# Graph sums on one Trainium2 core: the one-hot becomes the weights, and four chunks gather into one buffer

## The chip, the core and the metric

The kernel runs on one core of a Trainium2 chip. The core has five engines with their own instruction queues: TensorE for matrix products (PE; its weight loads are shown apart as PEld), VectorE (DVE), ScalarE (ACT), GpSimd (POOL) and SyncE (SP). PE reads SBUF and writes PSUM[...]. DMAs move data between HBM and SBUF. Engines wait for each other through semaphores.

The metric is the device time of one execution in microseconds (us), lower is better. Timed runs are made without the profiler; the profile is of one more execution.

## The reference

The reference is two layers of a graph network on 6250 nodes of 256 features. The edge list has 106,250 entries, sorted by destination; both directions of 50,000 random pairs and one loop for each node.

```python
xn = _layernorm(x)
x = x + _L0_gnn_ref(xn, edge_index, ...) + _L0_mix_ref(xn[None], ...)[0]   # two graph convolutions; linear attention
x = x + _L0_ffn_ref(_layernorm(x)[None], ...)[0]                           # 8 experts, the best one a node
xn = _layernorm(x)
x = x + _L1_gnn_ref(xn, ..., src, dst) + _L1_mix_ref(xn[None], ...)[0]      # mean of neighbours; attention and MLP
x = x + _L1_ffn_ref(_layernorm(x)[None], ...)[0]                            # shared MLP, 4 experts, the best two
```

Three times (two convolutions of layer 0, one mean in layer 1) it needs, for each node, the sum of the rows of its neighbours:

```python
msg = h[src] * norm[:, None]
out = jax.ops.segment_sum(msg, dst, num_segments=num_nodes)
```

In layer 0 a node's own row is added too (a second loop on top of the one in the edge list), and the sum is multiplied by a 256 x 256 matrix.

## The kernel before

**Tiles and chunks.** Nodes are held in 49 tiles of 128 (`NT`), 256 features each. Edges are worked on in 831 chunks of 128 (`NCH`), in the order of their destinations. As these are sorted, 17 chunks (`PER`) make up about one tile of destinations, and `base_of(c)` (L79) tells where chunk c's destinations should begin.

**Three passes.** `neighbour_sums` (L530) is called three times, at L826, L1148 and L1564, with the tables t1, t2, t3 in HBM. Each table has the nodes' rows in float32 (1 KB a row); t2 and t3 have them also as three bf16 parts that add up to the float32 value (1.5 KB a row). For each chunk POOL issues an indirect DMA (L542) that gathers the 128 source rows into SBUF, into `rows` or `parts`. Which of the two is settled by `is_f32` (L58): pass one is all float32; pass two has float32 in its first 136 chunks and in each third group of four after that, 367 in all; pass three in each fourth group, 208 chunks. Each chunk has a buffer of its own. `depth` tells how many there are: 12 float32 in pass one, 12 and 8 (bf16) in pass two, 6 and 10 in pass three.

**The one-hot.** For each group of four chunks (`OG`) DVE compares a row of numbers with the chunk's destinations `lof` (L549). The result has, for each edge, a one in the column of its destination, in a window of 84 nodes (`WIN`) that begins 38 (`MARG`) below `base_of(c)`.

**The products.** At L567 the gathered rows are the weights (128 edges by 128 features, two halves), and the one-hot is streamed through with its 84 columns. So the sums come out transposed: features on partitions, nodes on columns. A float32 chunk takes 2 products, a bf16 chunk 6. They add into a PSUM bank that covers one tile and 84 nodes of the next (`REACH`). As windows overlap freely, the bank is cleared first by a product with zeros (L560). In passes one and two the node's own rows are added by two products with the identity (L574), of a tile `own` that SP loads (L556).

**After a tile's last chunk** `whole` (L581) brings the bank into SBUF: ACT copies the part that only this tile's chunks reached (L587), DVE adds to the first 84 columns what the bank before had left over (L588), ACT keeps what belongs to the next tile (L592). The result is already transposed and goes as weights into the next product (`product`, L758, or the neigh product of `feed`, L1441).

**The order.** PE, POOL and SP run in the order in which the program is written; DVE and ACT are ordered by the compiler's scheduler. A planner, `pace` (L595), mixes other work into the three passes. It keeps a clock of its own: each chunk has a slot of 1.25 us, of which the sums are charged 0.45 (float32) or 0.23 (bf16) (L579), times a factor of 1.0 to 1.2. In the rest of the slot it places parts of other jobs. A job is a generator; `yield a, b` says that the part cost a of the slot's time and that the next may come b later. What is not placed by the last chunk is placed behind it by `rest()`. The jobs are:

- pass one: `settle1` (product and activation of a finished tile, which writes t2), the attention of layer 0 (`attention`), clearing of memory;
- pass two: `settle2`, `route` (gate of the 8 experts; scatters rows into `xs` by an indirect DMA on POOL, L947), `serve` (loads 1 MB of an expert's weights per chunk of 128 nodes, `hidden` and L1058, and scatters the result into `ys` on POOL, L1070), `back` (writes t3). Pass three cannot begin before t3 is complete;
- pass three: `mixing` (attention and MLP, fc1 and fc2), `feed` (mean of neighbours, experts, output).

The scatters into `xs` and `ys` stand in POOL's queue between the gathers. The first waits for slots from DVE, the second for y from DVE.

**The general branch.** If a destination lies outside its chunk's window (`far`, L422), a slow branch computes the sums another way. It decides at run time.

Of the kernel before, what the change touches and what calls it, by code (L numbers as in the profile page):

```python
# [31 lines left out]
F32 = mybir.dt.float32  # L33
# [21 lines left out]
FORMS = (1, 3, 4)  # L55


def is_f32(form, c):  # L58
    return c // OG % FORMS[form] == 0 or (form == 1 and c < 8 * PER)


# [12 lines left out]
MARG = 38  # L74
WIN = 84
# [7 lines left out]
def window(c):  # L83
    b = base_of(c) - MARG
    return max(b, 0), min(b + WIN, NPAD)


def tile_of(c):

    return window(c)[0] // P  # L90
# [3 lines left out]
REACH = P + WIN  # L94


OWN = (3, 13)
FINAL = [max(c for c in range(NCH) if tile_of(c) == t) for t in range(NT)]
AW = 7


def abase(c):

    return (base_of(c) - MARG) // 16
# [38 lines left out]
def gps_kernel(ctx: ExitStack, tc: tile.TileContext, i: dict, out: bass.AP):  # L143
# [57 lines left out]
    nc.vector.tensor_scalar(iota_w, iota_f, float(MARG), None, op0=ALU.subtract)  # L201
    iota_wf = consts.tile([P, P], F32, name="iota_wf")
    nc.vector.tensor_scalar(iota_wf, iota_f, float(MARG), None, op0=ALU.subtract)
    zrow = consts.tile([P, 512], BF16, name="zrow")
    nc.vector.memset(zrow, 0.0)
# [120 lines left out]
    with ExitStack() as st:  # L326
# [23 lines left out]
        for j in range(PER):  # L350
            nc.gpsimd.memset(offs[:, 0, j:j + 1], float(base_of(j)))
            nc.gpsimd.memset(offs[:, 1, j:j + 1], float(abase(j)))
# [6 lines left out]
        alo = alo.rearrange("p a b -> p (a b)")  # L359
        zb = prep.tile([P, 8 * NT], BF16, name="zb")  # L360
# [38 lines left out]
        for c0 in range(0, NCH, P):  # L399
# [7 lines left out]
            for c in range(c0, c0 + n):  # L407
                a, b = max(abase(c), 0), min(abase(c) + AW, 8 * NT)
                nc.tensor.matmul(dg[:, a:b], lhsT=ob[:, c - c0, :],
                                 rhs=oa[:, c - c0, a - abase(c):b - abase(c)],  # L410
                                 start=False, stop=(c == NCH - 1), skip_group_check=True)
# [13 lines left out]
        nc.vector.tensor_scalar(far[:, :NCH - 1], lof[:, :NCH - 1], WIN / 2.0 - MARG - 0.5, None, op0=ALU.subtract)  # L425
        nc.vector.tensor_scalar(far[:last, NCH - 1:], lof[:last, NCH - 1:], WIN / 2.0 - MARG - 0.5, None,
# [9 lines left out]
        nc.vector.tensor_scalar(fall, fall, WIN * WIN / 4.0, None, op0=ALU.is_gt)  # L436
# [93 lines left out]
    def neighbour_sums(tables, form, gp, after, own, other, depth=(8, 8)):  # L530
# [7 lines left out]
        for c in range(NCH):  # L538
            f32 = is_f32(form, c)
            g = gp.tile([P, C if f32 else 3 * C], F32 if f32 else BF16, name="rows" if f32 else "parts",  # L540
                        bufs=depth[0 if f32 else 1])
            nc.gpsimd.indirect_dma_start(  # L542
                out=g, out_offset=None, in_=(table if f32 else parts)[:, :],
                in_offset=bass.IndirectOffsetOnAxis(ap=sp[:, c:c + 1], axis=0))
            if c % OG == 0:
                n = min(OG, NCH - c)
                ohs = gp.tile([P, OG, WIN], F32 if f32 else BF16, name="onehotf" if f32 else "onehot",
                              bufs=4 if f32 and form < 2 else 3)
                nc.vector.tensor_tensor(ohs[:, :n, :],  # L549
                                        (iota_wf if f32 else iota_w)[:, None, :WIN].to_broadcast([P, n, WIN]),  # L550
                                        lof[:, c:c + n, None].to_broadcast([P, n, WIN]), op=ALU.is_equal)
            oh = ohs[:, c % OG, :]
            if own and c % PER == 0 and c // PER < NT:
                T = c // PER
                owns[T] = gp.tile([P, C], F32, name="own", bufs=2)
                nc.sync.dma_start(owns[T], table[T * P:(T + 1) * P, :])  # L556
            b = tile_of(c)
            if b not in ps:
                ps[b] = banks["pool"].tile([P, 512], F32, name="sums", tag="sum", bufs=2)
                nc.tensor.matmul(ps[b][:, :2 * REACH], lhsT=zrow[:, :P], rhs=zrow[:, :2 * REACH],  # L560
# [1025 lines left out]
```

## Time and profile before

| | us |
|---|---|
| timed runs, median of 3 (4121.96 to 4128.04) | 4127.97 |
| profiled execution | 4857.88 |
| its span, first to last instruction | 4856.1 |
| first gather | 98.7 |
| pass one, first to last gather | 98.7 to 1315.4 |
| pass two | 1339.5 to 2885.4 |
| pass three | 3306.7 to 4746.5 |

The profiled execution is 730 us longer than the timed ones. The granted TensorE clock is 0.815 on average, lowest in pass one. How the page shows the stages, in 40 slices of 121 us, in tenths:

```profile
PE   3787557567576567758667678865778877878878
POOL 2666666666555565555555541104555555555550
PEclk9898676666667678878788789987888888998989
DMA  4455334333332354444444543655333333333330
```

A digit is the busy share of the slice (for PEclk the granted clock, for DMA the mean of 16 engines). The three stretches of 5 and 6 in POOL's row are the passes.

In the lists of instructions, a float32 product shows as two records, a bf16 product as one. `x5624` is the number of records; the number behind the bar is the time in which at least one was running, then the mean of one, then the idle time of the engine before them with what ended it. A wait put down to "remote" ended by a signal that the profile ties to no instruction near it.

### The profile page before, as it was taken

What the parts mean: (1) busy time and instruction counts of PE and PEld (TensorE: products, weight loads), DVE (VectorE), ACT (ScalarE), POOL (GpSimd) and SP (SyncE); (2) the same over time, 40 slices, a digit from 0 to 9 for tenths busy, and PEclk for the clock granted to TensorE, in tenths of its full rate; (3) what the DMA queues carried; (4) which work ended last, traced back from release to release, by engine and by line L of the source; (5) the groups of instructions that cost most, each with busy time, mean ns of one, the idle gap of its engine ahead of it and who ended that gap; (6) DMA issues with size and microseconds to landing.
All of it is one profiled execution on the core that took longest, in us unless ns stands there. A gap on an engine that the chain in (4) does not pass through costs nothing. (4 is left out here: it accounts for less than half of the span.)

```text
span 4856.1 us, 59500 instructions
## 1 busy us (share of the span) xinstructions
PE 3463.1 (71%) x22273; PEld 2860.7 (59%) x22273; DVE 1422.3 (29%) x5275; ACT 957.1 (20%) x2026; POOL 2532.2 (52%) x2665
## 2 busy tenths in 40 slices
PE   3787557567576567758667678865778877878878
PEld 2677446556565455646555456654666666666666
DVE  5312112122212222222122311733333333333333
ACT  3111000000001112212222133530112211211212
POOL 2666666666555565555555541104555555555550
PEclk9898676666667678878788789987888888998989
DMA  4455334333332354444444543655333333333330
GB/s 150 137 161 153 112 114 117 114 113 115 109 91 84 104 158 136 137 147 121 150 142 128 161 122 114 210 192 147 110 113 111 106 108 106 109 111 109 105 111 19
DMA packets 332191, 601.89 MB, mean 124 GB/s; under 512 B 57498, under 2 KB 230341, under 8 KB 331888
## 3 DMA queue, kind: packets, MB, share of 16 engines
q0 software_dynamic: 142672, 412.98, 29.5%
q1 hardware_dynamic: 188366, 184.56, 12.4%
q8 instruction: 176, 2.88, 0.2%
q14 instruction: 127, 1.04, 0.1%
q10 hardware_dynamic: 850, 0.43, 0.0%
HBM read 521.95 MB, written 75.80 MB: 123 GB/s over the span
## 5 line engine op out<-in xcount | busy, mean ns | idle before, releaser
L567 PE MATMUL sums<-onehotf,rows 128*128 128x84 f32 (+2 forms) x5624 | 937.8, 313 | 273.8 <-issue 92.5
L567 PEld LDWEIGHTS sums<-onehotf,rows 128*128 128x128 f32 x5624 | 909.5, 230 | 378.9 <-issue 201.3
L542 POOL DMA_INDIRECT rows<-t1f,sp x831 | 807.7, 972 | 498.7 <-issue 159.6
L542 POOL DMA_INDIRECT parts<-t3b,sp x623 | 600.0, 963 | 575.9 <-PE sums L567 325.5
L567 PEld LDWEIGHTS <-parts 128*128 128x128 bf16 x6522 | 408.3, 108 | 368.5 <-DMA parts<-t2b,sp 165.6
L567 PE MATMUL sums<-onehot,parts 128*128 128x84 bf16 x6522 | 474.4, 216 | 183.5 <-DMA parts<-t2b,sp 144.0
L542 POOL DMA_INDIRECT parts<-t2b,sp x464 | 446.6, 963 | 270.2 <-PE sums L567 98.4
L884 PE MATMUL hid<-ft,fw 128*128 128x256 f32 (+1 forms) x1824 | 522.4, 424 | 41.8 <-ACT ht L886 32.7
L549 DVE TENSOR_TENSOR onehotf<-iota_wf,lof 128x336 f32<-128x336 f32 x352 | 178.3, 508 | 1030.9 <-PE sums L567 510.5
L542 POOL DMA_INDIRECT rows<-t2f,sp x367 | 350.6, 955 | 144.8 <-issue 98.5
L884 PEld LDWEIGHTS hid<-ft,fw 128*128 128x128 f32 x1824 | 353.5, 211 | 96.6 <-ACT ht L886 39.1
L762 PE MATMUL h<-w,aggt 128*128 128x256 f32 x392 | 155.6, 535 | 238.7 <-issue 154.2
L1070 POOL DMA_INDIRECT ys<-y,to x64 | 63.9, 998 | 496.9 <-DVE y L1063 209.0
L886 ACT ACTIVATE ht<-hid,fb 128x256 f32<-128x256 f32 (+1 forms) x456 | 208.4, 471 | 458.5 <-PE hid L884 239.1
L1058 PE MATMUL exp<-wd,ht 128*128 128x256 f32 x1024 | 274.0, 408 | 5.8 <-ACT ht L886 3.6
L549 DVE TENSOR_TENSOR onehot<-iota_w,lof 128x336 bf16<-128x336 bf16 x272 | 137.1, 505 | 478.6 <-PE sums L567 225.6
L762 PEld LDWEIGHTS h<-w,aggt 128*128 128x128 f32 x392 | 92.5, 261 | 261.7 <-issue 162.3
L542 POOL DMA_INDIRECT rows<-t3f,sp x208 | 201.0, 966 | 63.2 <-issue 61.4
L1058 PEld LDWEIGHTS exp<-wd,ht 128*128 128x128 f32 x1024 | 194.3, 202 | 34.4 <-ACT ht L886 5.8
L587 ACT COPY aggt<-sums 128x88 f32<-128x88 f32 x96 | 22.3, 232 | 893.7 <-remote 422.5
L1411 PE MATMUL fc_ps<-fc,ut 128*128 128x256 f32 x588 | 166.5, 408 | 9.3 <-issue 9.1
L1399 PE MATMUL fc_ps<-ht,fc 128*128 128x256 f32 (+1 forms) x600 | 163.3, 395 | 2.0 <-issue 1.9
(356 smaller groups left out, 4540.9 us busy)
## 6 DMA issues: line engine op xcount, KB each, us to landing
wd<-in_L_ffn_Wd SPq DMA_DIRECT2D x64, 1024.0 KB
xs<-zero SPq DMA_DIRECT2D x8, 1799.0 KB
rows<-t1f,sp POOLq DMA_INDIRECT x831
parts<-t3b,sp POOLq DMA_INDIRECT x623
t2b<-t2s SPq DMA_DIRECT2D x49, 192.0 KB
t3b<-t3s SPq DMA_DIRECT2D x24, 384.0 KB
fs<-xs SPq DMA_DIRECT2D x64, 128.5 KB
bd<-in_L_ffn_bd SPq DMA_DIRECT2D x64, 128.0 KB
```

What stands on the lines that cost most here:

```text
L542: nc.gpsimd.indirect_dma_start(out=g, out_offset=None, in_=(table if f32 else parts)[:, :], in_offset=bass.IndirectOffsetOnAxis(ap=sp[:, c ...
L549: nc.vector.tensor_tensor(ohs[:, :n, :], (iota_wf if f32 else iota_w)[:, None, :WIN].to_broadcast([P, n, WIN]), lof[:, c:c + n, None].to_b ...
L567: nc.tensor.matmul(ps[b][:, h, n0 - b * P:n1 - b * P], lhsT=g[:, k * C + h * P:k * C + (h + 1) * P], rhs=oh[:, n0 - w0:n1 - w0], start=Fal ...
L587: nc.scalar.copy(dst[:, :, WIN:], sums[:, :, WIN:P])
L762: nc.tensor.matmul(h, lhsT=at[:, k, :], rhs=w[:, k, :], start=(k == 0), stop=(k == 1))
L884: nc.tensor.matmul(h_ps[:, :w], lhsT=fw1[:, k, m * P:(m + 1) * P], rhs=ft[:, k, :w], start=(k == 0), stop=(k == 1))
L886: nc.scalar.activation(ht[:, m, :w], h_ps[:, :w], AF.Gelu, bias=fb1[:, m:m + 1], scale=1.0)
L1058: nc.tensor.matmul(y_ps, lhsT=ht[:, m, q * P:(q + 1) * P], rhs=wd[:, m, :], start=(m == 0), stop=(m == 7))
L1070: nc.gpsimd.indirect_dma_start(out=ys[v][:, :], out_offset=bass.IndirectOffsetOnAxis(ap=to, axis=0), in_=y, in_offset=None)
L1399: nc.tensor.matmul(u_ps[:, :w], lhsT=fc1[:, k, m * P:(m + 1) * P], rhs=ht[:, k, :w], start=(k == 0), stop=(k == 1))
L1411: nc.tensor.matmul(h_ps, lhsT=ut[:, m, t * P:(t + 1) * P], rhs=fc2[:, m, :], start=False, stop=(m == 5))
```

## The change

The roles of rows and one-hot are exchanged, and the groups are gathered as a whole.

- A chunk's one-hot is 128 edges by 128 nodes and is the weight; the gathered rows are streamed through, 256 columns at a time. The sums come out with nodes on partitions. A float32 chunk takes one product, a bf16 chunk three (with the same weights).
- A chunk's stretch of 128 nodes begins at a multiple of 64. A PSUM bank has two halves of 256 columns: one for the tile's own stretch, one for the stretch that begins 64 nodes later. The first chunk of a stretch starts its accumulation, so that no product with zeros is needed.
- `whole` adds up the pieces with DVE and ACT, adds the own rows there (`own` is no longer a product), and `turn` transposes the tile by two PE transposes and an ACT copy before it goes on as weights. `settle1`, `settle2` and `feed` have a step for that, with 0.45 a tile in the planner's clock.
- Four chunks gather into one tile of SBUF, with four indirect DMAs issued together at the group's first chunk. `depth` counts such groups: 4 in pass one, 3 in passes two and three. The buffer comes free when the fourth chunk is done.
- Pass one is all float32, passes two and three are all bf16.
- The planner is charged 0.43 for a float32 chunk and 0.33 for a bf16 chunk.
- The offsets of the stretches need 12 more memsets on POOL before pass one; the window of the degree count is one column wider; the general branch is adapted. Pass one's buffers are in a pool of their own, which is closed after it.

```diff
-FORMS = (1, 3, 4)
 def is_f32(form, c):
-    return c // OG % FORMS[form] == 0 or (form == 1 and c < 8 * PER)
+    return form == 0
...
-MARG = 38
-WIN = 84
+HALF = P // 2
+BELOW = 60
...
 def window(c):
-    b = base_of(c) - MARG
-    return max(b, 0), min(b + WIN, NPAD)
+    return min(max((base_of(c) - BELOW + HALF // 2) // HALF * HALF, 0), (NT - 1) * P)
...
-            g = gp.tile([P, C if f32 else 3 * C], F32 if f32 else BF16, name="rows" if f32 else "parts",
-                        bufs=depth[0 if f32 else 1])
-            nc.gpsimd.indirect_dma_start(
-                out=g, out_offset=None, in_=(table if f32 else parts)[:, :],
-                in_offset=bass.IndirectOffsetOnAxis(ap=sp[:, c:c + 1], axis=0))
             if c % OG == 0:
                 n = min(OG, NCH - c)
-                ohs = gp.tile([P, OG, WIN], F32 if f32 else BF16, name="onehotf" if f32 else "onehot",
-                              bufs=4 if f32 and form < 2 else 3)
+                gs = gp.tile([P, OG, C if f32 else 3 * C], F32 if f32 else BF16, name="rows" if f32 else "parts",
+                             bufs=depth)
+                for j in range(n):
+                    nc.gpsimd.indirect_dma_start(
+                        out=gs[:, j, :], out_offset=None, in_=(table if f32 else parts)[:, :],
+                        in_offset=bass.IndirectOffsetOnAxis(ap=sp[:, c + j:c + j + 1], axis=0))
+                ohs = gp.tile([P, OG, P], F32 if f32 else BF16, name="onehotf" if f32 else "onehot", bufs=3)
...
-            for h in range(2):
-                for k in range(1 if f32 else 3):
-                    nc.tensor.matmul(ps[b][:, h, n0 - b * P:n1 - b * P],
-                                     lhsT=g[:, k * C + h * P:k * C + (h + 1) * P], rhs=oh[:, n0 - w0:n1 - w0],
-                                     start=False, stop=True, skip_group_check=True)
-            if own and c % PER == 8 and c // PER < NT:
-                T = c // PER
-                mine = owns.pop(T)
-                for h in range(2):
-                    nc.tensor.matmul(ps[T][:, h, :P], lhsT=mine[:, h * P:(h + 1) * P], rhs=ident,
-                                     start=False, stop=True, skip_group_check=True)
+            h = C * (window(c) // HALF % 2)
+            parts_n = 1 if f32 else 3
+            for k in range(parts_n):
+                nc.tensor.matmul(ps[b][:, h:h + C], lhsT=ohs[:, c % OG, :], rhs=g[:, k * C:(k + 1) * C],
+                                 start=(c in FIRST and k == 0), stop=(c in LASTS and k == parts_n - 1))
...
-            other(c, 0.45 if f32 else 0.23)
+            other(c, 0.43 if f32 else 0.33)
...
-    def whole(dst, sums, begun, last):
+    def whole(dst, sums, begun, own, last):
...
+        if own is None:
+            nc.scalar.copy(dst, sums[:, :C])
         else:
-            nc.scalar.copy(dst[:, :, WIN:], sums[:, :, WIN:P])
-            nc.vector.tensor_tensor(dst[:, :, :WIN], sums[:, :, :WIN], begun, op=ALU.add)
...
+            nc.vector.tensor_tensor(dst, own, sums[:, :C], op=ALU.add)
+        left = None
+        if not last:
+            left = gp.tile([P, C], F32, name="left", bufs=2)
+            nc.scalar.copy(left[:HALF, :], sums[HALF:, C:])
+            nc.vector.tensor_tensor(dst[HALF:, :], dst[HALF:, :], sums[:HALF, C:], op=ALU.add)
+        if begun is not None:
+            nc.vector.tensor_tensor(dst[:HALF, :], dst[:HALF, :], begun[:HALF, :], op=ALU.add)
         return left
+
+    def turn(at, agg):
+        tr = ps_tr("aggtr")
+        for k in range(2):
+            nc.tensor.transpose(tr[:, k * P:(k + 1) * P], agg[:, k * P:(k + 1) * P], ident)
+        nc.scalar.copy(at, tr[:, :C].rearrange("p (k n) -> p k n", k=2))
...
+    def settle1(T, agg):
+        yield 0.0, 2.5
         at = gp.tile([P, 2, P], F32, name="aggt", bufs=2)
+        turn(at, agg)
+        summed.pop(0)
+        yield 0.45, 1.0
...
-        neighbour_sums(t1, 0, gp, after1, True, other, depth=(12, 0))
+        neighbour_sums(t1, 0, gp, after1, True, other, depth=4)
...
-        neighbour_sums(t2, 1, gp, after2, True, other, depth=(12, 8))
+        neighbour_sums(t2, 1, gp, after2, True, other, depth=3)
...
-        at = agt[t0 // 2]
+        at = work.tile([P, 2, 2, P], F32, name="agt", bufs=2)
+        for t in range(n):
+            turn(at[:, t, :, :], agt[t0 // 2][:, t, :])
+        del agt[t0 // 2]
+        yield 0.45 * n, 1.0
...
-        neighbour_sums(t3, 2, gp, after3, False, other, depth=(6, 10))
+        neighbour_sums(t3, 2, gp, after3, False, other, depth=3)
```

## The prediction

> **What bounds the kernel now.** I read the page's busy line first, then the gathers' own line of code, then windows by stage, then the timeline inside a stage, and last the rows by shape.
>
> ```profile
> PE 3463.1 (71%) x22273; PEld 2860.7 (59%) x22273; DVE 1422.3 (29%) x5275; ACT 957.1 (20%) x2026; POOL 2532.2 (52%) x2665
> ...
> L542 POOL DMA_INDIRECT rows<-t1f,sp x831: 940/946/1390, 98.7 to 1315.4; - x167
> L542 POOL DMA_INDIRECT parts<-t3b,sp x623: 940/946/1278, 3313.0 to 4746.5; - x156
> L542 POOL DMA_INDIRECT parts<-t2b,sp x464: 940/946/1311, 1562.6 to 2881.7; - x155
> L542 POOL DMA_INDIRECT rows<-t2f,sp x367: 940/946/1270, 1339.5 to 2885.4; - x184
> L542 POOL DMA_INDIRECT rows<-t3f,sp x208: 942/946/2023, 3306.7 to 4724.9; - x104
> ```
>
> No engine is near full by busy time. But the gathers give three passes of 831: 98.7 to 1315.4 (1217 us), 1339.5 to 2885.4 (1546 us), 3306.7 to 4746.5 (1440 us). Everything else is 98.7 before, 24 and 421 between, 110 after: 654 us. The timeline tells what paces a pass:
>
> ```profile
> 691.49 0.94 POOL L542 DMA_INDIRECT rows<-t1f,sp  x1 [0.30 <-remote]
> 692.73 0.95 POOL L542 DMA_INDIRECT rows<-t1f,sp  x1 [0.30 <-issue]
> 693.98 0.95 POOL L542 DMA_INDIRECT rows<-t1f,sp  x1 [0.30 <-issue]
> ...
> 699.93 0.23 ACT L587 COPY aggt<-sums 128x88 f32<-128x88 f32 x1 [18.32 <-remote]
> ...
> 700.58 2.07 PE L762 MATMUL h<-w,aggt 128*128 128x256 f32 x4 [11.06 <-DVE aggt L588]
> ...
> 690.00:695.00 5.00, 0.00 (x0) 0.00 (x0) 0.00 (x0) 0.00 (x0) 3.78 (x4) 0.57 0.37 105
> 695.00:700.00 5.00, 0.00 (x0) 0.00 (x0) 0.51 (x1) 0.07 (x1) 2.98 (x3) 0.50 0.27 79
> ```
>
> A gather is 0.95 us and is followed by 0.30 us whatever it waits for, so POOL needs 1.25 us for each: 831 x 1.25 = 1039 us a pass, 3116 us for three. The profiled passes are 1087 us over that. The last four lines show why I don't take these 1087 us at their word: PE has run all its matmuls by 690 and idles at half clock, yet ACT and POOL are told of them one by one until 699.9. In this execution PE's signals come late. Its own time is 4857.88 us (span 4856.1 and 1.8 around it), 730 more than the median of the timed runs, 4127.97. If the 654 us outside the passes are the same without the profiler, the timed passes take 4128 - 656 = 3472 us, 356 over POOL's floor. So the timed kernel is bound by POOL's gathers in the passes and by PE and its chains in the two tails, where no gather runs:
>
> ```profile
> 2890.00:3310.00 420.00, 309.87 (x1379) 242.09 (x1378) 173.56 (x837) 166.16 (x348) 46.96 (x50) 0.90 0.51 163
> ...
> 4760.00:4856.00 96.00, 75.39 (x355) 62.53 (x353) 37.05 (x149) 29.20 (x57) 0.00 (x0) 0.91 0.03 10
> ```
>
> The sums below are made on the profiled stages; where a stage is a pass I say what of it I believe is left in timed runs, and I add the result to the median.
>
> **What the Trainium skill says.** "TensorE: Matmul & The Clock Gate", section "Back-to-back issue gap": a warm matmul of 256 columns takes 262 cycles, 109 ns. No bf16 matmul of 256 columns is in this trace; twelve float32 records of that width take 2.84 us (0.24 each, or 0.22 without the last one's drain: twice the figure, as for two passes). The same page, table at its head: PE takes weight loads ahead, GpSimd is a strict FIFO. The trace agrees: the ys scatters hold the gathers behind them. "DMA: Bandwidth & Descriptors", "Anatomy of one DMA": about 2 us fixed per DMA; here a gather issued at 2007.75 let PE go at 2015.35, beside two loads of 1 MB. "ScalarE: Activation LUTs", "What ACT_TABLE_LOAD costs": 1283 ns; the trace has 1283.
>
> **The change part by part.**
>
> ```profile
> L567 PE MATMUL sums<-onehotf,rows 128*128 128x84 f32 x5536 | 920.4, 312 | 198.9 <-issue 92.1 <-DMA rows<-t2f,sp 68.1 <-DMA rows<-t1f,sp 35.1
> L567 PE MATMUL sums<-onehot,parts 128*128 128x84 bf16 x6492 | 472.6, 216 | 183.5 <-DMA parts<-t2b,sp 144.0 <-issue 38.4
> L549 DVE TENSOR_TENSOR onehotf<-iota_wf,lof 128x336 f32<-128x336 f32 x350 | 177.4, 508 | 1018.8 <-PE sums L567 498.3 <-remote 380.5 <-issue 63.0
> ...
> L947 POOL DMA_INDIRECT xs<-f,slots x40 | 40.6, 1016 | 78.1 <-DVE slots L943 40.3 <-issue 18.5 <-DMA xs<-f,slots 10.1
> L1070 POOL DMA_INDIRECT ys<-y,to x31 | 31.2, 1008 | 192.4 <-DVE y L1063 74.8 <-DVE run L933 71.4 <-DVE pf L984 21.2
> ```
>
> (1) PE's products. Warm, a timeline row has 56 float32 records of 84 columns in 6.38 us, 0.114 each, four a chunk: 0.46 us; six bf16 ones 0.39 us with the last one's drain, I take 0.23. Before: 1406 float32 chunks x 0.46 + 1087 x 0.23 = 647 + 250 = 897, with 147 clearing products (0.18) and 392 records for own rows (0.114): 968 us. After: 831 chunks x 2 x 0.22 = 366, 1662 x 3 x 0.109 = 543, 294 transposes at 0.11 to 0.25 = 32 to 73: about 960. So 26% fewer instructions but no less array time. Both lie under POOL's 1.25 us a chunk: 0.
>
> (2) The gathers' number and pace stay: 0. They carry more: 367 + 208 = 575 chunks go from 131 to 197 KB, 38 MB in all. Below nothing is excluded. If all of it were uncovered at the 123 GB/s of the page it would be 306 us; POOL's pace covers it except where 1 MB loads run beside it. I take 10, in the second pass.
>
> (3) Four gathers stand together at the group's first chunk. In the built order a ys scatter follows its expert product by 2.4 chunks before, 3.9 after: PE's operands for it were asked for 1.5 x 1.25 = 1.9 us earlier relative to the scatter. The profiled second pass has 270 us of scatter waits (last two rows), about 30 of them long. 30 x 1.9 = 57; bounds 0 (PE late for another reason) and 95 (all 50 scatters or pairs). Fewer scatters in the pass, 28 and 38 for 31 and 40: 5 x 1.3 = 6. I take -56.
>
> (4) Buffers: 20 and 16 single ones become 12 in three groups, freed by the fourth chunk, so POOL may lead PE by 8 to 12 chunks, 10 to 15 us. PE's waits for DMA reach 9 us in the second pass. 0 to 40; I take 10. The first pass goes from 12 to 16: 0.
>
> (5) DVE and ACT. A one-hot is 512 instead of 336 elements: 508 ns becomes 0.69 to 0.77 us, 624 of them, +110 to +165 us of DVE, which is 29% busy: hidden. A tile's sums pass three more short DVE operations, two transposes and an ACT copy, some 2 us, before its product; the planner leaves 2.5 + 1.0 there. It is bare only at the end of pass one: +2. In pass three the transposes share one PSUM buffer with all others and wait for ACT's copy, about 1 us twice for 25 feeds in a pass where PE is the nearest second: 0 to 50, I take 20. Table loads rise from 226 to 268 (30 to 70 at the gelu of L1401): 42 x 1.28 = 54 us of ACT, mostly idle; I take 5. Twelve memsets of 88 ns on POOL lie in its 88.8 us wait.
>
> (6) The order. The planner charges 0.33 for a bf16 chunk where it charged 0.23 or 0.45, and 0.45 a tile for the transposes. So other work is placed later. In the built order PE has 741 matmuls between the last sum of pass two and the first of pass three before, 821 after; behind the last sum of pass three 188 before, 352 after (two more mixings and feeds). Nothing covers these: the gathers are over. First tail: 420 us for 741; 80 x 310/741 (PE busy) = 33, 80 x 420/741 = 45. I take 38. Second: 96 us for 188; 164 x 75/188 = 66, 164 x 96/188 = 84. I take 72. The passes they leave don't get shorter, since POOL paces them.
>
> Sum: 10 - 56 + 10 + 2 + 20 + 5 + 38 + 72 = +101, of which the pass terms (-9) are unsure in size and sign. 4128 + 101 = 4229; I take 4220, since the tails' extra work can overlap a little better than the work there now.
>
> **Rivals.**
> A. The passes are bound by PE's stream of instructions and its late signals in timed runs too. For it: POOL waits 567 us for sums at L542 in the profile, and a quarter of PE's instructions go. Against: the timed kernel is 730 us shorter, so little of that is left. If most of the 356 us over the floor fell (-220), with (3) and the tails: 4128 - 220 - 56 + 110 + 20 = 3982; with half of that 4090. It decides once the passes lose over 110 us, the tails' price. This is the faster side.
> B. The tails are repaid: pass three is PE's, not POOL's (it has some 930 to 940 us of PE work against 1039), so work put off shortens it. Then of the second tail only the 45 us remain by which PE's total in stage three grows: 4128 + 38 + 45 - 56 + 20 = 4175; if the first tail is repaid too, about 4137.
> C. Gathers become late: 12 buffers and 197 KB with the 1 MB loads beside them. Half of the 306 us of (2) with the 40 of (4) shows: 4229 + 140 + 30 = 4400; a quarter, 4325.
> D. The fixed stretch doesn't hold the nodes and the general branch runs. The inputs' sorted destinations lie at 0 to 117 of each stretch of 128: excluded.
>
> **Numbers.** My forecast 0.60, A 0.19 (4090 and below), B 0.09, C 0.12. What this kernel's measurement can tell from no change is about 0.2%, 8 us. Slower: forecast, C, and most of B: 0.77. Same: 0.04 from B and the edge of A. Faster: 0.19. The range drops half of A and the upper half of C: 4090 to 4325. The forecast's own is 4160 to 4280.
>
> **What would show it.** In the changed profile: gathers again every 1.25 us; PE matmul records about 16,600 with array time in the sums nearly the same; the profiled span may fall by more than the timed run, as fewer PE signals are late (so its passes must not be read alone). Step 6: time from the last gather of pass two to the first of pass three 421 + 38, from the last gather to the end 110 + 72. Step 3: ys and xs waits in pass two down from 270 towards 200. I am wrong if the tails have not grown, or if the passes lose more than 110 us in timed runs; C is seen as PE idle ended by DMA of parts in passes two and three.

## The result, and the profile after

| | us | runs |
|---|---|---|
| before, median | 4126.1 (4121.96 to 4128.04) | timed beside it |
| after, median | 4324.33 (4313.78 to 4331.61) | 4 |
| ratio | 1.048 [1.0456, 1.0504] | |

The changed kernel is 198 us slower. The forecast was 4220, which is 94 us slower.

Chips differ in this work: the kernel before takes 4113 to 4126 us on some and about 4875 us on another, so times are compared on one chip only, as ratios. The profile of before shown ahead of the prediction (4857.88 us, granted clock 0.815) looks like the slower kind: the timed runs there take 4854 to 4896 us at 0.816 to 0.822. So I took one more profile of it on a chip where it takes 4116 us. That one, not the first, stands beside the profile of after. Here are its gathers, from the view of one line's instructions (count, shortest/median/longest in ns, first and last start in us):

```profile
L542 POOL DMA_INDIRECT rows<-t1f,sp x831: 940/946/1378, 99.2 to 1164.0; - x167
L542 POOL DMA_INDIRECT parts<-t3b,sp x623: 940/946/1460, 2902.1 to 4008.3; - x156
L542 POOL DMA_INDIRECT parts<-t2b,sp x464: 942/946/1283, 1362.3 to 2467.8; - x155
L542 POOL DMA_INDIRECT rows<-t2f,sp x367: 942/946/1280, 1182.2 to 2471.5; - x184
L542 POOL DMA_INDIRECT rows<-t3f,sp x208: 942/946/2022, 2895.8 to 3993.8; - x104
```

And the same view of the changed kernel:

```profile
L542 POOL DMA_INDIRECT rows<-t1f,sp x831: 940/946/1472, 99.4 to 1181.2; - x167
L542 POOL DMA_INDIRECT parts<-t2b,sp x831: 942/946/1602, 1201.6 to 2429.4; - x167
L542 POOL DMA_INDIRECT parts<-t3b,sp x831: 942/946/1632, 2874.4 to 4139.5; - x167
```

The median gather takes the same 946 ns with 131 KB and with 197 KB. The first and last starts give the stages of both. A pass goes from its first to its last gather; the first tail is what lies between passes two and three, the second what lies behind pass three:

| stage, us | before (span 4118.0) | after (span 4312.0) | difference |
|---|---|---|---|
| ahead of the first gather | 99.2 | 99.4 | 0 |
| pass one | 1064.8 | 1081.8 | +17 |
| between | 18.2 | 20.4 | +2 |
| pass two | 1289.3 | 1227.8 | -62 |
| first tail | 424.3 | 445.0 | +21 |
| pass three | 1112.5 | 1265.1 | +153 |
| second tail | 109.6 | 172.5 | +63 |

The differences add up to the spans' 194 us. The changed kernel profiled once more, on the same chip as this profile of before, gives +22, -56, +25, +157 and +65 for the passes and tails in their order. The tails were forecast at +38 and +72. What was not forecast is pass three. The page of after shows where in it the time goes, in the last quarter of POOL's row of 40 slices (108 us each), where POOL gathers only about half as often, and PE's clock sinks with it:

```profile
POOL 1777777777767777777776411137777776544410
PEclk9999777777767798888897999979999999887789
```

POOL issues the gathers, and waits for nothing else in that stretch but the products. From the view of waits of after, 3500 to 4140 us (engine, tile and line waiting, for what; us in total, times, longest):

```profile
POOL parts L542 <- PE sums L560: 207.0, 11, 34.7
```

Nine of these eleven hold 202 us, less the 0.30 us that follows every gather anyway. They come every 55 to 76 us, once for each pair of tiles. The timeline of PE around the end of one of them, and under it POOL's:

```profile
3886.57 1.03 PE L1536 MATMUL ffn<-ew,e2t 128*128 128x256 f32 x4
3887.43 1.89 PE L1370 MATMUL att<-wf,xnt 128*128 128x256 f32 x8
3889.16 0.38 PE L587 MATMUL aggtr<-ident,agg 128*128 128x128 f32 x2
3890.01 0.44 PE L587 MATMUL aggtr<-ident,agg 128*128 128x128 f32 x2 [0.47 <-ACT agt L588]
3890.28 3.77 PE L560 MATMUL sums<-parts,onehot 128*128 128x256 bf16 x33
3894.74 0.49 PE L560 MATMUL sums<-parts,onehot 128*128 128x256 bf16 x3 [0.70 <-DMA parts<-t3b,sp]
```

```profile
3891.70 0.95 POOL L542 DMA_INDIRECT parts<-t3b,sp  x1 [30.89 <-PE sums L560]
3892.95 0.94 POOL L542 DMA_INDIRECT parts<-t3b,sp  x1 [0.30 <-issue]
```

Before 3890 PE does products of experts, mixing and feed, at full clock, and no sums: from 3860 to 3892 it is busy 30.3 of 32 us. All this while the 12 gather buffers are full, so POOL stands still for 30.89 us. Then PE takes eleven chunks in one go (33 records in 3.77 us), POOL starts again, and now PE waits for each gather. First one engine stands and then the other.

The lumps stand in the order of the program. In the trace of after nine stretches between two chunks' sums in pass three take 14 to 42 us, filled with other PE products; the longest such stretch in before takes 4.3 us. The code that makes them is unchanged: `after3` runs the planner's `step` for as long as more than two pairs of sums are waiting for `feed` (`while len(agt) > 2`). As I read it, with the new charges `feed` is always behind, so that this loop, once a pair, runs a whole lump.

### The profile page after: what moved, and what is told of

It reads as the page before. It is cut to its first block, busy times and chain, and to the rows that moved or that the text cites. A ratio compares the mean times of both kernels' runs of the same rounds, so it can differ in the third digit from the quotient of the medians.

```text
span 4312.0 us, 47268 instructions
## 1 busy us (share of the span) xinstructions
PE 3340.2 (77%) x16530; PEld 2425.5 (56%) x16530; DVE 1661.0 (39%) x5515; ACT 1064.4 (25%) x2117; POOL 2568.3 (60%) x2677
## 5 line engine op out<-in xcount | busy, mean ns | idle before, releaser
L560 PE MATMUL sums<-parts,onehot 128*128 128x256 bf16 x4986 | 891.6, 302 | 436.7 <-DMA parts<-t2b,sp 269.5
L542 POOL DMA_INDIRECT parts<-t3b,sp x831 | 807.4, 972 | 458.0 <-issue 223.0
L542 POOL DMA_INDIRECT parts<-t2b,sp x831 | 810.4, 975 | 274.8 <-issue 230.7
L560 PEld LDWEIGHTS <-onehot 128*128 128x128 bf16 x4986 | 518.4, 106 | 756.1 <-issue 556.7
L560 PE MATMUL sums<-rows,onehotf 128*128 128x256 f32 x1662 | 648.1, 503 | 283.1 <-DMA rows<-t1f,sp 225.5
L560 PEld LDWEIGHTS sums<-rows,onehotf 128*128 128x128 f32 x1662 | 337.9, 235 | 537.8 <-DMA rows<-t1f,sp 365.3
L546 DVE TENSOR_TENSOR onehot<-iota_w,lof 128x512 bf16<-128x512 bf16 x416 | 286.3, 689 | 602.9 <-PE sums L560 595.8
L546 DVE TENSOR_TENSOR onehotf<-iota_f,lof 128x512 f32<-128x512 f32 x208 | 144.0, 692 | 438.0 <-PE sums L560 433.4
L1393 PEld LDWEIGHTS fc_ps<-ht,fc 128*128 128x128 f32 x600 | 113.8, 211 | 25.9 <-DVE e1t L1501 6.5
L1405 PEld LDWEIGHTS fc_ps<-fc,ut 128*128 128x128 f32 x588 | 106.6, 191 | 12.4
```

Source lines behind the costliest of these rows:

```text
L542: nc.gpsimd.indirect_dma_start(out=gs[:, j, :], out_offset=None, in_=(table if f32 else parts)[:, :], in_offset=bass.IndirectOffsetOnAxis( ...
L546: nc.vector.tensor_tensor(ohs[:, :n, :], (iota_f if f32 else iota_w)[:, None, :].to_broadcast([P, n, P]), lof[:, c:c + n, None].to_broadca ...
L560: nc.tensor.matmul(ps[b][:, h:h + C], lhsT=ohs[:, c % OG, :], rhs=g[:, k * C:(k + 1) * C], start=(c in FIRST and k == 0), stop=(c in LASTS ...
L1393: nc.tensor.matmul(u_ps[:, :w], lhsT=fc1[:, k, m * P:(m + 1) * P], rhs=ht[:, k, :w], start=(k == 0), stop=(k == 1))
L1405: nc.tensor.matmul(h_ps, lhsT=ut[:, m, t * P:(t + 1) * P], rhs=fc2[:, m, :], start=False, stop=(m == 5))
```

## The experiments

Fourteen runs in four groups: the first group on a chip of the slower kind, groups two to four on one and the same quicker chip, where the kernel before takes 4113 to 4117 us.

### Pass three's charges as they were, and the other way round (first group)

Before, on this chip: 4874.88 (4854 to 4896).

In the changed kernel, pass three's charge and `feed`'s step for the transposes:

```diff
-            other(c, 0.43 if f32 else 0.33)
+            other(c, (0.43, 0.33, 0.23)[form])
...
-        yield 0.45 * n, 1.0
+        yield 0.0, 1.0
```

> The changed kernel with pass three's charges of the kernel before: 0.23 for a bf16 chunk and nothing for the transposes; the rest as changed. In the built order the nine lumps of 12 to 30 us of other PE work between two chunks of pass three are gone, and 201 matmuls instead of 351 stand behind its last sum. Theory 1, the planner's charges make lumps that block POOL, and the longer tail: the nine waits of POOL (202 us in the profile) vanish and the tail goes from 172 to about 112, so 4324 - 202 - 60 = 4060, with some new waits 4060 to 4140. Theory 2, PE has no room for the work in pass three (982 us of array work against 1039): the same waiting comes back spread out, 4250 to 4324.

Measured: 4653.27, ratio 0.9548 [0.9508, 0.9588]. With the old charges in pass two and in `settle1` and `settle2` as well:

```diff
-            other(c, 0.43 if f32 else 0.33)
+            other(c, 0.43 if f32 else 0.23)
...
-        yield 0.45, 1.0
+        yield 0.0, 1.0
```

> The changed kernel with the charges of the kernel before in passes two and three. As the run with pass three alone, and behind pass two stand 656 matmuls instead of 820. Theory 1: the first tail shortens by 164 x 0.45 = 74 us and pass two stays POOL's, so another 50 to 75 less: 3990 to 4080. Theory 2: pass two cannot take the work: as the run with pass three alone or slower.

Measured: 4675.08, ratio 0.9575 [0.9530, 0.9620]. The first tail fell by 70 us, and pass two grew by 82. Then the kernel before with the new charges, in pass three alone:

```diff
-            other(c, 0.45 if f32 else 0.23)
+            other(c, 0.33 if form == 2 else 0.45 if f32 else 0.23)
...
         at = agt[t0 // 2]
+        yield 0.45 * n, 1.0
```

> The kernel before with pass three's charges of the changed one (0.33 a chunk, 0.45 a tile). In its built order nine lumps of 10 to 30 us appear and 333 matmuls instead of 187 stand behind the last sum. Theory 1: 150 to 190 for the lumps (it has 16 buffers where the changed has 12, so somewhat less blocking) and 60 for the tail: 4126 + 210 to 250 = 4330 to 4380. Theory 2: order is not what costs: 4120 to 4190.

Measured: 5078.59, ratio 1.0409 [1.0364, 1.0453], so 204 us more. And with the new charges everywhere:

```diff
-            other(c, 0.45 if f32 else 0.23)
+            other(c, 0.43 if form == 0 else 0.33)
...
-        yield 0.0, 1.5
+        yield 0.45, 1.5
...
         at = agt[t0 // 2]
+        yield 0.45 * n, 1.0
```

> The kernel before with the changed one's charges in all passes. As the run before it, and 821 matmuls instead of 740 behind pass two. Theory 1: another 25 to 45: 4360 to 4420. Theory 2: 4120 to 4200.

Measured: 5092.78, ratio 1.0437 [1.0391, 1.0484]. In the profile of before with pass three's new charges (waits, 3290 to 4920 us) the long waits are there, with the old products and the old buffers:

```profile
POOL parts L542 <- PE sums L567: 490.4, 157, 36.0
```

In before on such a chip the same row (3300 to 4750 us) has 325.5 us and none over 8.7. Pass three went from 1440 to 1604 us and the second tail from 110 to 164. So with the old products, too, the charges alone make the lumps and the longer tail.

### The same on the quicker kind of chip (second group)

The first group leaves open what the charges cost where the result was measured, so the changed kernel and its version with pass three's old charges ran once more, together.

> The changed kernel once more, unaltered, beside the kernel before and beside the version with pass three's old charges, all on one chip. Theory 1 (lumps of other work inside pass three, 202 us of POOL waits, and 60 us of tail; both a matter of the order): the changed kernel is 262 us longer than the version with pass three's old charges, whatever the chip. On a chip where the kernel before takes about 4126 the ratio to it is 1.048; on one where it takes about 4875 it is (4653 + 262) / 4875 = 1.008. Theory 2 (the new form of the products and gathers itself costs time in the passes): the changed kernel is at most 100 us longer than that version, and about 1.03 or less above it in ratio.

> The changed kernel with the planner's charges of pass three as they were (0.23 a chunk, nothing for the turn). Theory 1: 262 us below the changed kernel on the same chip. Where the kernel before takes 4126 that is 4062, ratio 0.984; where it takes 4875 it is 0.955 again. Its pass three has no POOL wait over 8 us and takes about 1065 us, its second tail 112 us. Theory 2: less than 100 us below the changed kernel, so above the kernel before where that takes 4126 (4224 or more, ratio 1.024).

Measured, beside before at 4116.91: the changed kernel 4330.11, ratio 1.0501 [1.0468, 1.0533]; with pass three's old charges 4219.39, ratio 1.0235 [1.0204, 1.0265]. The charges of pass three cost 110 us, not the 262 that I had taken from the length of the waits and of the tail. The gathers of the version with the old charges:

```profile
L542 POOL DMA_INDIRECT rows<-t1f,sp x831: 942/947/1457, 99.1 to 1187.6; - x167
L542 POOL DMA_INDIRECT parts<-t2b,sp x831: 942/947/1578, 1208.4 to 2437.2; - x167
L542 POOL DMA_INDIRECT parts<-t3b,sp x831: 941/947/1932, 2887.5 to 4102.9; - x167
```

No wait is over 5 us any more and the second tail is 117 us, but pass three still takes 1215 us, 103 more than in before. Theory 1 falls in its size: most of the 202 us is not the lumps' own. Taking out 202 us of waits shortened the pass by 50 (54 beside the changed kernel's second profile), because something else then holds it nearly as long. The two theories had put the boundary at 100 us, and 110 fits neither well.

### Groups and bytes (second group)

```diff
+            g = gp.tile([P, C if f32 else 3 * C], F32 if f32 else BF16, name="rows" if f32 else "parts",
+                        bufs=4 * depth)
+            nc.gpsimd.indirect_dma_start(
+                out=g, out_offset=None, in_=(table if f32 else parts)[:, :],
+                in_offset=bass.IndirectOffsetOnAxis(ap=sp[:, c:c + 1], axis=0))
...
-                gs = gp.tile([P, OG, C if f32 else 3 * C], F32 if f32 else BF16, name="rows" if f32 else "parts",
-                             bufs=depth)
...
-            g = gs[:, c % OG, :]
```

> The version with pass three's old charges, with the grouped gathers undone: each chunk gathers into a buffer of its own, issued at its own chunk, with the same number of buffers (16, 12, 12). The order of PE's work is the same. Prediction's steps 3 and 4: grouping brings 56 us in pass two by shorter waits of the scatters and costs 10 us for buffers freed late, so this is 46 us longer than with the groups (scatter waits in pass two from 82 back to about 138 us). Rival: the groups only hold buffers longer; then this is 0 to 40 us shorter, at POOL waits for sums at the gather.

Measured: 4237.28, ratio 1.0276 [1.0243, 1.0310], beside 1.0235 [1.0204, 1.0265] with groups. The intervals overlap; at its middle the grouping is worth 17 us. Pass two is 1236.1 us for 1228.8, pass three the same to 0.1 us. The scatters' rows in pass two say the same (in the list by line, the number behind the second bar is POOL's idle time ahead of them). Before, then the version without groups, then the one with:

```profile
L947 POOL DMA_INDIRECT xs<-f,slots x40 | 41.0, 1024 | 31.4 <-DMA xs<-f,slots 11.5 <-issue 8.1 <-DVE none L988 6.3
L1070 POOL DMA_INDIRECT ys<-y,to x31 | 31.3, 1009 | 135.1 <-DVE run L933 52.0 <-DVE y L1063 42.9 <-DVE pf L984 18.9
```

```profile
L944 POOL DMA_INDIRECT xs<-f,slots x38 | 38.2, 1005 | 19.2 <-DMA xs<-f,slots 9.4 <-issue 3.7 <-DVE slots L940 1.7
L1067 POOL DMA_INDIRECT ys<-y,to x29 | 30.3, 1046 | 84.0 <-DVE y L1060 27.0 <-DVE run L930 21.6 <-DVE ones_e L237 13.4
```

```profile
L947 POOL DMA_INDIRECT xs<-f,slots x38 | 40.0, 1053 | 33.6 <-DMA xs<-f,slots 26.3 <-issue 5.8 <-DVE none L990 0.3
L1070 POOL DMA_INDIRECT ys<-y,to x29 | 29.4, 1015 | 53.6 <-DVE run L933 19.9 <-issue 7.0 <-DVE y L1063 6.8
```

The sums are 166.5, 103.2 and 87.2 us. Grouping takes 16 us of scatter waits away, not 57; most of the fall from 166.5 was there without it.

```diff
 def is_f32(form, c):
-    return form == 0
+    return form < 2
```

> The version with pass three's old charges, with pass two gathering float32 rows (131 KB a gather and one float32 product a chunk for 197 KB and three bf16 products); the order of all other work is the same. It takes 831 x 66 KB = 54 MB out of pass two and adds 83 us to PE's array time in it by the tile shapes. Step 2 of the prediction (bytes cost little): pass two shortens by 0 to 15 us. Rival (gathers of parts come late and hold PE): pass two shortens by 50 us or more. Third (PE's work in the pass counts): pass two grows by up to 80 us.

Measured: 4264.64, ratio 1.0343 [1.0310, 1.0376]. With 54 MB less to gather and 83 us more of PE's array time pass two is 1283.4 us, 55 more. So PE's time counts in pass two as well. What fewer bytes bring can't be told apart here: 28 us, if the 83 counted in full; less, if not.

### What holds pass three (third group)

> The kernel before, unaltered, for a profile on a chip where it takes about 4117 us: time ratio 1. There the passes must take 4117 less 98.7 + 20 + 421 + 110 = 3467 us. With pass one near 1090 two passes are left with about 2377, against 1233 + 1270 in the changed kernel. Theory 1a (PE's time in the products counts in pass three, where PE is 91% busy in the version with pass three's old charges): pass three is shorter than that version's 1215 us by the tile shapes' difference, 272 - 229 = 43, so about 1170, and pass two about 1205. Theory 1b (POOL's waits for scatters count): pass three equals 1215 within 15 and pass two is about 1160.

Measured: 4115.96, ratio 1.0005 [0.9997, 1.0014]; its profile is the one in the section on the result. Pass three is 1112.5 us. Windows inside the pass, of before and then of the version with pass three's old charges (length, then busy us and count of PE, PE's weight loads, DVE, ACT, POOL, then the clock):

```profile
2950.00:3950.00 1000.00, 934.96 (x7332) 793.24 (x7331) 451.04 (x1561) 264.57 (x544) 719.79 (x748) 0.97 0.50 141
```

```profile
2960.00:4080.00 1120.00, 1015.03 (x5621) 812.66 (x5619) 521.12 (x1632) 342.19 (x633) 772.33 (x763) 0.93 0.50 140
```

PE is busy 93% of the time in before. A chunk (one gather in POOL's count) takes 1.25 us of PE's busy time there, and 1.33 in the new form; PE is idle for 0.09 and 0.14 us a chunk. Over the 731 chunks behind the first hundred that is 59 + 37 = 96 us, nearly all of the 103. The lower clock in the new form (0.93 for 0.97) is not the reason: most of its other float32 products of 256 columns take 380 ns a record, for some 393 in before. The chain of work that ended last, followed back through pass three of before (what released each step is inferred from the signals), lies on PE for 921 us, on DVE for 158 and on POOL for 5. So pass three was PE's before the change, not POOL's. The sums' rows over the whole pass, in the list by line and shape, name a part of PE's busy time. Before:

```profile
L567 PE MATMUL sums<-onehot,parts 128*128 128x84 bf16 x3666 | 236.1, 203 | 3.0 <-DMA parts<-t3b,sp 3.0
...
L567 PE MATMUL sums<-onehotf,rows 128*128 128x84 f32 x816 | 119.4, 276 | 0.0
...
L560 PE MATMUL sums<-zrow 128*128 128x424 bf16 x47 | 16.5, 352 | 0.0
```

The new form with the old charges (of its one wait of 62 us for a gather, 55 lie in the tail ahead of the pass):

```profile
L560 PE MATMUL sums<-parts,onehot 128*128 128x256 bf16 x2466 | 409.2, 284 | 63.3 <-DMA parts<-t3b,sp 63.2
...
L587 PE MATMUL aggtr<-ident,agg 128*128 128x128 f32 x88 | 18.0, 286 | 10.2 <-ACT agt L588 10.2
```

236.1 + 119.4 + 16.5 = 372 us against 409 and 18 for the transposes. Little more than half the records, and 55 us more busy. But the chain tells another part of it. In the new form with the old charges it lies on PE for 923 us, hardly more than before, on DVE for 227 (69 more, some 16 of them in the one-hots) and on ACT for 19 (14 more). The three other runs of this form with the transposes have PE at 921 to 943 and DVE at 227 to 229. No run takes DVE's work out, so how the 103 us divide between the products and what PE waits for from DVE stays open. To see whether PE's time really sets the pass, I took two of its three products out:

```diff
-            parts_n = 1 if f32 else 3
+            parts_n = 1 if form != 1 else 3
```

> The version with pass three's old charges, in pass three with the first of a chunk's three bf16 products alone: two thirds of the neighbour sums' products there are left out (so the sums have bf16's accuracy), the gathers and their bytes stay. It takes 181 us of PE array time by the tile shapes out of pass three. Theory 1a (PE bounds pass three): pass three falls from 1215 to between 1040 and 1090, close to POOL's floor of 1039, and the time falls by 125 to 175 us. Rival (chains and signals bound it, not PE's array time): it falls by less than 60 us.

Measured: 4087.86, ratio 0.9933 [0.9916, 0.9950]. Pass three fell by 125 us to 1090.7, at the edge of what theory 1a expected. The chain's part on PE fell by 134 us to 789, and DVE's is 237. So PE's time in the products counts in this pass; that says what taking it out is worth, not what the change added. What holds the pass at 1090.7 is not shown: the gathers with their 0.30 us fill 1068 us of it, but the chain runs through PE and DVE. Next, the planner's charges in pass two:

> The changed kernel with the planner's charges in passes two and three as they were. Against the version with pass three's old charges alone, 58 us of PE work by the tile shapes go from the first tail into pass two. Step 6 of the prediction (pass two is POOL's, so work put off is not repaid): the first tail falls by 67 us and pass two grows by less than 20, so 50 us or more below 4219 where the kernel before takes 4117. Rival (repaid, as on the chip of the slower kind, +82 for -70): within 20 us of 4219.

Measured: 4225.98, ratio 1.0271 [1.0249, 1.0293]. The first tail fell from 450.3 to 370.8 us and pass two rose from 1228.8 to 1328.9: repaid in full. The scatters' waits in pass two are 128.6 (ys) and 48.1 us (xs), 177 in all for 87. So it was the charge, which keeps other work out of pass two, that shortened the scatters' waits.

The last of the group is made from the kernel before:

```diff
-    return c // OG % FORMS[form] == 0 or (form == 1 and c < 8 * PER)
+    return (form < 2 and c // OG % FORMS[form] == 0) or (form == 1 and c < 8 * PER)
...
-        neighbour_sums(t3, 2, gp, after3, False, other, depth=(6, 10))
+        neighbour_sums(t3, 2, gp, after3, False, other, depth=(0, 14))
```

> The kernel before with all chunks of pass three as bf16 products of 84 columns (14 gather buffers): PE's sums in pass three take 187 us by the tile shapes for 229, more bytes are gathered (197 KB for 131 in 208 chunks), and the planner, charged 0.23 for every chunk, puts another 34 us of other work from the second tail into the pass. Theory 1a (PE bounds pass three): the pass changes by 35 - 42 = -7, the tail by -45, time 40 to 60 us below the kernel before. Rival (bytes or buffers bound it): no faster than before.

Measured: 4103.59, ratio 0.9968 [0.9952, 0.9983]. That is 0.3% below the kernel before, 9 us by the medians and 13 by the ratio, where 40 to 60 were expected. The second tail is 68 us for 110, as expected; pass three is 1136.8, so 24 longer instead of 7 shorter. The traces of the pass say where the saving went: the sums with their clearing are busy for 326 us instead of 364, but the other products, of which the lower charge places more in the pass, for 961 instead of 907 (the two overlap). All in all PE is busy for 13 us more and idle for 11 more.

### Transposes or products (fourth group)

```diff
-            turn(at[:, t, :, :], agt[t0 // 2][:, t, :])
+            nc.scalar.copy(at[:, t, :, :], agt[t0 // 2][:, t, :].rearrange("p (k n) -> p k n", k=2))
```

> The version with pass three's old charges, without the two PE transposes a tile in pass three: an ACT copy takes the sums as they stand (so the weights of the products with them are not transposed, and the output differs). Pass three is 1215 us there and 1112 us in the kernel before, for the same other work. If the 103 us are PE's time, this gives back the transposes' busy 18 us, the 10 us in which they wait for ACT's copy, and what the second in line waits for: 25 to 45 us, and the products' own 36 us of busy time and the rest stay. If the transposes' shared PSUM buffer is the main cost (a chain, not PE's time), 60 to 100 us go.

Measured: 4188.24, ratio 1.0168 [1.0127, 1.0209], which is 0.0067 or 28 us below the version with the transposes; pass three 1194.3 for 1215.4, 21 us. The intervals of the times just touch, but the pass was 1213.0 to 1215.4 us in all four runs with the transposes. So the transposes are a fifth of the 103 us, and what remains, 82 us, comes with the products and the DVE and ACT work around them, not told apart.

And the kernel before with fewer float32 products in pass two too (pass three as in the last run of the third group):

```diff
-    return c // OG % FORMS[form] == 0 or (form == 1 and c < 8 * PER)
+    return form == 0 or (form == 1 and c < 8 * PER)
```

> The kernel before with its products of 84 columns, all bf16 in pass three (14 buffers) and all bf16 in pass two after the first eight tiles (8 buffers as before). By the tile shapes 47 us of sums leave pass two and the planner puts 29 us of other work from the first tail in their place; the tail loses 83 matmuls. If PE's time counts in pass two as in pass three: pass two about even, first tail 424 to about 380, second tail 68, so about 4065 where the kernel before takes 4115, ratio 0.988. If 8 buffers or the bytes bind pass two, it grows by 40 us or more and the ratio is 0.997 or above.

Measured: 4114.69, ratio 0.9995 [0.9980, 1.0009]: no change. The first tail is 384 us for 424, the second 68 for 110, but pass two is 1341.9 for 1289.3 and pass three 1136.5 for 1112.5. What leaves the tails comes back in the passes once more.

## Why the prediction was right and wrong

The sign was right, and the tails grew as forecast, if by less. The size was not: +94 for +198. Three profiles, each with one step more of the change, sort the 198 us by cause:

| stage, us | before | new form, all old charges | new charges in pass two | the change |
|---|---|---|---|---|
| pass one | 1064.8 | 1076.4 | 1088.5 | 1081.8 |
| pass two | 1289.3 | 1328.9 | 1228.8 | 1227.8 |
| first tail | 424.3 | 370.8 | 450.3 | 445.0 |
| pass three | 1112.5 | 1213.0 | 1215.4 | 1265.1 |
| second tail | 109.6 | 117.1 | 117.1 | 172.5 |
| timed, ratio | 1 | 1.0271 | 1.0235 | 1.048 |

From the first column to the second, the new form costs 108 us of span, 100 of them in pass three. (Pass two and the first tail also trade work there: "old charges" means 0.23 for every bf16 chunk, where before had 367 float32 chunks at 0.45, so that 656 matmuls stand behind pass two for 740.) From the second to the third nothing is gained or lost beyond what the intervals allow. From the third to the fourth pass three's charges cost 92 us (110 in the timed runs that stood side by side).

- **What bounds the kernel** is where it failed first. I put the 730 us between the profile and the timed runs down to that one execution ("In this execution PE's signals come late"). The same kernel takes 4854 to 4896 us in timed runs on the chip of the first group, so such a time needs no odd execution: the 730 us go with the chip. Taking them for one execution's oddity left no length for the timed passes but a mean, 3472 us for all three together and "356 over POOL's floor", and with it the verdict "bound by POOL's gathers in the passes". The three are 1065, 1289 and 1113 us, and in the third PE is busy 93% of the time.
- **Step 1** (products, 0) failed by that: "Both lie under POOL's 1.25 us a chunk". The array time of 968 and 960 us was a sum over all passes, where a gain in pass one hid a loss in pass three: there the prediction's own prices give 208 x 0.46 + 623 x 0.23 = 239 us before and 831 x 0.327 = 272 after. The trace has 372 and 409 busy, and with the work around them, without the transposes, the pass grew by 82 us. This is the largest term of what was missing; what share the products themselves have in it is open.
- **Step 2** (bytes, +10): not seen apart from PE's time.
- **Step 3** (groups, -56, though its own terms, 57 and 6, add to 63): the waits of the scatters fell from 166.5 to 83.1 us, and yet not by this step. Groups bring 16 of it (17 us in the timed middle, step 4's +10 included); keeping work out of pass two brings 90, and the first tail pays for that. A right number for a wrong reason.
- **Step 5**: the transposes' 20 us in pass three are 21 in the pass and 28 in the time. That DVE's longer one-hots are "hidden" because DVE is 29% busy does not follow: the chain through pass three has 69 us more of DVE in the new form, some 16 of them one-hots. What the pass would gain without them isn't shown. The rest wasn't separated.
- **Step 6** (+38 and +72): measured +21 and +63 between the two kernels. Against the old charges in the same form it is +80 and +55, so the count of matmuls (164 and 150 fewer behind the last sum) gave the tails well. Two things beside them were missed. "The passes they leave don't get shorter, since POOL paces them" is wrong: pass two gave back 100 us for 80. And I counted only what lies behind the last sum, not how the work left in pass three is spread: the pass lost 230 of its 3643 records of other PE products and got longer by 50 us, because the loop in `after3` turned the backlog into lumps.
- **Rivals.** B's ground, that pass three is PE's, was right; I had priced PE there by tile shapes at 930 to 940 us, where it is 1034 busy, and so let 1039 of POOL win, itself no more than the gathers' least time. Its conclusion, that put-off work is repaid, holds in pass two and was undone by the lumps in pass three. A (passes bound by PE's late signals) is not seen on the quicker chips. On the slower kind the version with pass three's old charges is 4.5% faster than before; the change itself wasn't run there.

Pass one's 17 us more (12 to 24 in the other runs), which no step forecast, are the gathers themselves. Before and after, from the pages:

```profile
L542 POOL DMA_INDIRECT rows<-t1f,sp x831 | 802.7, 966 | 352.5 <-issue 149.3
L542 POOL DMA_INDIRECT rows<-t1f,sp x831 | 822.6, 990 | 349.2 <-issue 228.1
```

They are busy 20 us more in all, and the idle time between them is 3 us less. The median is the same 946 ns; the mean rises from 966 to 990. The slow ones run beside a one-hot on DVE: 235 such gathers take 1.00 us on average before and 252 take 1.07 us after, all others 0.95 in both, and a one-hot takes 0.69 us for 0.51. That the longer one-hots slow the gathers is likely, but not shown: no run changes them alone.

## What to carry to other kernels

Bound each stage by itself: divide each engine's busy time by that stage's chunks and set it beside the pacing engine's step, before an edit's cost is called hidden. A sum over stages can be even while the stage that binds gets longer. Nor does a small busy share make an engine's work hidden: what counts is whether the engine that binds waits for it. When a planner's charge is raised, count not only what moves behind the loop but the largest stretch of other work between two steps of it: once that is longer than the buffers last (12 gathers of 1.25 us here, 15 us, against stretches of up to 42), the engines take turns standing still.

## What was not expected of the hardware

One kernel, with the same instructions, in two profiles on two chips. The version with pass three's old charges on the chip of the first group:

```profile
L542 POOL DMA_INDIRECT rows<-t1f,sp x831: 940/946/1457, 99.8 to 1301.1; - x167
L542 POOL DMA_INDIRECT parts<-t2b,sp x831: 940/946/1602, 1321.6 to 2749.2; - x167
L542 POOL DMA_INDIRECT parts<-t3b,sp x831: 940/946/1498, 3202.0 to 4531.5; - x167
```

Its passes are 1201, 1428 and 1329 us, against 1088, 1229 and 1215 in the second group; the first tail is 453 for 450 and the second 116 for 117. A gather's 946 ns is the same too. What differs are PE's signals in the passes: on the slower chip 63%, 43% and 35% of the matmuls that signal have no signal on record within 0.3 us of their end (63%, 40% and 45% in before), and at most 2% in the tails; on the quicker one it is about 1% or less anywhere. Part of that share are missing records: the slower chip's trace has 2994 signals for 3563 such matmuls. The cause isn't in the traces, nor whether it is the chip or a state that it was in. The new form has a quarter fewer matmuls and a fifth fewer signals, and that version's ratio to before is 0.9548 on one chip and 1.0235 on the other: which of two kernels is the quicker depended on the chip.

Products of 256 bf16 columns came at 3.77 / 33 = 0.114 us in the row shown above; the Trainium skill ("TensorE: Matmul & The Clock Gate", "Back-to-back issue gap") has 262 cycles for 256 columns, 109 ns, and the row includes the last one's drain. Fed one chunk at a time, three of them take 0.49 us instead of 0.34.
